# A last 1x1 convolution in seven block products, one engine for the sample copies, and a reordered opening

## The chip, the core and the metric

The kernel runs on one core of a Trainium2 chip: TensorE (PE; its weight loads are PEld) for matmuls, VectorE (DVE), ScalarE (ACT) and GpSimd (POOL) for the rest, SyncE (SP) to issue DMAs. The metric is the device time of one execution in microseconds. Each engine works through its own queue in order and waits there for semaphores.

## The reference

Two bottleneck layers run on x of 64 images, 1024 channels, 14x14, in float32.

```python
# layer 0
out = relu(bn(conv(x, w1)))                  # 1024 -> 256, 1x1
out = relu(bn(conv(out, w2, pad=1)))         # 256 -> 256, 3x3
out = bn(conv(out, w3))                      # 256 -> 1024, 1x1
x   = relu(x + softplus(residual_scale) * out)
# layer 1: a deformable bottleneck with group norms (32 groups)
out = relu(group_norm(conv(x, w1)))          # 1024 -> 256, 1x1
om  = conv(out, w_off, pad=1) + b_off        # 27: nine offsets x, nine y, nine masks
py, px = grid_y + om[9:18], grid_x + om[:9]
sampled = bilinear_sample(out, py, px) * sigmoid(om[18:])   # for each of 9 taps
out = einsum('bckhw,ock->bohw', sampled, w2)
out = relu(group_norm(out))
out = group_norm(conv(out, w3))              # 256 -> 1024, 1x1
return relu(out + x)
```

Layer 0 normalises over the batch, so each of its convolutions must be done before the next; layer 1 normalises inside one image.

## The kernel before

Images go in pairs (NP = 32 pairs, N2 = 392 = 2 x 196 columns). Channels lie on the 128 partitions: 1024 channels are CB = 8 blocks, 256 are MB = 2. The first layer is three stages over the whole batch and ends at about 967 us; nothing of it is changed.

The second layer (`build_second_bottleneck`) works on pairs in slots. Slot t holds the sampling and second convolution of pair t, the first convolution, first norm, offset convolution and sampling weights of pair t+1, and the second norm, third convolution, third norm and store of pair t-1. `slot(t)` writes out the order of TensorE's work by hand: `put(steps, extra, at)` inserts extra steps ahead of numbered steps, `weave(a, b)` mixes two lists evenly. The other engines' orders are made by a planner from the same list, except where `keep_in_program_order` holds an instruction in place.

The stages, as the steps of the list name them:

- `first_conv` (L1038): 16 products for a pair; ScalarE copies the two banks out (L1046) and VectorE takes statistics (L936). `first_norm` sums groups on TensorE (L960, L979), takes the power -0.5 on GpSimd (L985), makes scale and shift on VectorE (L991 to L1001), rectifies on ScalarE (L1062), and GpSimd copies into `pad` (L1069).
- `offset_conv` (L1082): 18 products in four column groups into one bank, added up by ScalarE and VectorE (L1092 to L1097). `selection` makes the mask, and sends offsets and mask through DRAM, so that they come back spread over taps and rows. `factors` makes the one-dimensional weights of the bilinear sampling (L1139 to L1146) and sends them out. `spread` brings them back as S and X (DMAs, L1212 and L1216), and `corners` multiplies the two on VectorE (L1234).
- `transposes` (L1175) puts the rectified rows on the partitions as aT; `lend` copies the part that the middle rows share by DMA.
- `sampling` (L1252): for each of two tap sets (five taps and four), three groups of rows, two channel blocks and one or two images, matmuls of S with aT. A bank holds up to 420 columns; two banks (`ps_s`) take turns. Each bank is copied to sm: even turns by ScalarE (L1264), odd ones by VectorE (L1262).
- `second_conv` (L1285): 36 products for a pair (72 passes in the trace), over both tap sets into two banks. `second_norm` is the first norm's twin with the rectification at L1314, in place in h2.
- `third_conv` (L1342): eight output blocks, each two products of 392 columns; ScalarE copies the bank to z (L1351), VectorE takes statistics. `third_norm` and `finish` end with z*scale + y on VectorE (L1373) and the rectification on ScalarE (L1381); `store` writes z out.
- `residual` (L212, L221) ends the first layer for pair t+2.

The banks of the third convolution, first convolution, offset convolution and transposes come from one pool of three (`ps`), in turn. S, X, sm, aT, z and h2 come from the pool `two`, of two buffers for each tag. `fill()` opens the second layer: first convolutions of pairs 0, 1 and 2, with the weights of pairs 0 and 1 as far as the slots that follow need them. `tail()` ends the last pair.

Of the kernel before, what the change touches and what calls it, by code (L numbers as in the profile page):

```python
# [16 lines left out]
P = 128  # L17
# [5 lines left out]
MB = 2  # L23
# [21 lines left out]
def kernel(  # L45
# [830 lines left out]
    def build_second_bottleneck(l1, path, run, early):  # L876
        groups, R, tapsets = path.groups, path.rows, path.tapsets
        QR = R * W
        starts = sorted({r0 for _, _, chunks in groups for r0 in chunks})
        KT = max(k1 - k0 for k0, k1 in tapsets)  # L880
        wide = sum((h1 - h0) * W * 2 * len(chunks) for h0, h1, chunks in groups)
        NS = len(starts)

# [283 lines left out]
        def transposes(p):  # L1167
            q = pairs[p]

            def step(i, c):  # L1170
                if i == c == 0:
                    q["aT"] = two.tile([QR, 2, MB, NS, P], FP, tag="aT", name=f"aT_{p}")
                pt = ps.tile([QR, 2, P], FP, tag="ps", name=f"tr_{p}_{i}_{c}")
                for j, r0 in enumerate((starts[0], starts[-1])):
                    nc.tensor.transpose(  # L1175
                        pt[:, j, :], q["a1"][:, c, ds(i * HW + r0 * W, QR)], ident
                    )
                nc.vector.tensor_copy(q["aT"][:, i, c, :: NS - 1], pt)

            return [lambda i=i, c=c: step(i, c) for i in range(2) for c in range(MB)]  # L1180
# [57 lines left out]
        def sampling(p, e):  # L1238

            q = pairs[p]  # L1240
            k0, k1 = tapsets[e]
            kt = k1 - k0
            out = []

            def step(turn, g, h0, h1, chunks, c, i0, ni):
                if turn == 0:
                    q["sm"][e] = two.tile([P, MB, KT, 2, HW], FP, tag="sm", name=f"sm_{p}_{e}")
                n = (h1 - h0) * W
                pt = ps_s.tile([P, ni, kt, n], FP, tag="ps_s", name=f"sp_{p}_{e}_{g}_{c}_{i0}")
                for i in range(ni):  # L1250
                    for j, r0 in enumerate(chunks):
                        nc.tensor.matmul(  # L1252
                            pt[:, i],
                            q["aT"][:, i0 + i, c, starts.index(r0), :],
                            q["S"][e][g, r0][:, :, i0 + i, :],
                            start=(j == 0),
                            stop=(j == len(chunks) - 1),
                        )
                for i in range(ni):
                    dst = q["sm"][e][:, c, :kt, i0 + i, h0 * W : h1 * W]  # L1260
                    if turn % 2:
                        nc.vector.tensor_copy(dst, pt[:, i])  # L1262
                    else:
                        nc.scalar.copy(dst, pt[:, i])  # L1264
# [41 lines left out]
        def second_norm(p):  # L1306
            q = pairs[p]

            def end():
                n = q["gn2"]  # L1310
                n.finish()
                for c in range(MB):
                    for i in range(2):
                        nc.scalar.activation(  # L1314
                            q["h2"][:, c, ts(i, HW)],
                            q["h2"][:, c, ts(i, HW)],
                            AF.Relu,
                            bias=n.sh[:, c, i : i + 1],
                            scale=n.sc[:, c, i : i + 1],
                        )  # L1320

            return [lambda: q["gn2"].mean(), end]

        def parts(p):

            return ((0, 4), (4, 6), (6, 8)) if p == NP - 1 else ((0, CB),)

        def third_conv(p):
            q = pairs[p]

            def step(o, c):
                half, b = divmod(o, HB)
                if o == c == 0:
                    q["z"] = []
                    q["gn3"] = [
                        Norm(b1 - b0, 1, N3S, N3B, f"gn3_{p}_{b0}", b0) for b0, b1 in parts(p)
                    ]
                if b == c == 0:
                    q["z"].append(two.tile([P, HB, N2], FP, tag="z", name=f"z_{p}_{half}"))
                if c == 0:  # L1340
                    q["pt3"] = ps.tile([P, N2], FP, tag="ps", name=f"d3_{p}_{o}")
                nc.tensor.matmul(  # L1342
                    q["pt3"],
                    w3b_sb[:, c, ts(o, P)],
                    q["h2"][:, c, :],
                    start=(c == 0),
                    stop=(c == MB - 1),
                )
                if c == MB - 1:
                    z = q["z"][half][:, b, :]  # L1350
                    nc.scalar.copy(z, q["pt3"])  # L1351
                    n = [n for n in q["gn3"] if n.b0 <= o][-1]
                    n.stats(o - n.b0, z)

            return [lambda o=o, c=c: step(o, c) for o in range(CB) for c in range(MB)]

# [55 lines left out]
        def slot(t):  # L1412
# [27 lines left out]
            om = part(front, offset_conv, t + 1) + part(front, selection, t + 1)  # L1440
            om_at = (2,) * (MB * T) + (4,)
            if d1:
                todo = put(d1, norm2 + weights[:1], (4, 8, 10) if back else (10,))
                todo += put(weave(sp[0], d3[: 2 * HB]), norm1 + weights[1:], (4, 9, 12))
                todo += put(weave(sp[1], d3[2 * HB :]), om, om_at)
            else:
                todo = weights[:1]
                todo += put(sp[0], norm2 + weights[1:], (2, 6, 7) if back else (7,))
                todo += put(weave(sp[1], d3[: 2 * HB]), norm1, (1, 4))
                todo += put(d3[2 * HB :], om, om_at)  # L1450
# [9 lines left out]
            if front:  # L1460
# [7 lines left out]
        def tail():  # L1468

            p = NP - 1  # L1470
            for step in second_norm(p):
                step()
            d3 = third_conv(p)

            def products(first, end):
                for step in d3[first:end]:
# [157 lines left out]
```

## Time and profile before

| | us |
|---|---|
| median of three runs | 3069.08 (3066.68 to 3069.61) |
| the profiled execution, its own time | 3069.61 |
| its span in the trace | 3067.7 |
| second layer's opening, to the first full slot | 967 to 1130 |
| slots 2 to 30 | 1130 to 2970 |
| last slot and tail | 2970 to 3068 |

The span is the stretch between the first and the last traced instruction. In the rows of groups and of the timeline, "x" is a count and a matmul of float32 operands stands as two passes; a bracket tells how long the engine was idle just before and what ended that. The ends of TensorE's rows are modelled, so differences of starts are the better measure of what a matmul costs.

### The profile page before, as it was taken

To read this page: it belongs to the slowest core of one execution; us is meant where nothing else is said; L and a number is where in the kernel's file an instruction comes from. 1 tells how busy PE (TensorE), PEld (TensorE's weight loads), DVE (VectorE), ACT (ScalarE), POOL (GpSimd) and SP (SyncE) were. 2 spreads that over 40 slices of the span, in tenths; PEclk is the share of its full clock that TensorE was granted. 3 is DMA by queue.
4 is the path that set the end of the run, shared out by engine and by line. 5 is a ranking of instruction groups with operands and counts; after the bars stand their busy time and mean duration, and the time that the engine had idled before them with its cause. 6 is when DMAs were issued, how large, how long until landed. Compare 5 with 4: busy or idle time off the path is not lost.

```text
span 3067.7 us, 33283 instructions
## 1 busy us (share of the span) xinstructions
PE 2985.4 (97%) x10521; PEld 1718.6 (56%) x10521; DVE 1988.7 (65%) x5321; ACT 1113.2 (36%) x2367; POOL 695.2 (23%) x631
## 2 busy tenths in 40 slices
PE   9999999989999799999999999999999999999997
PEld 5555555545555455555555555555555555555554
DVE  7877999988887355555555555555555555555554
ACT  0000212215554244443444434444344444444433
POOL 4621566646663010010000101010010100101000
PEclk9999999999999999999999999999999999999998
DMA  7654000025554444455544554445544455444531
GB/s 229 192 171 125 14 1 0 1 91 217 217 215 147 147 127 128 137 162 168 165 129 140 162 172 156 134 143 160 174 148 135 147 161 179 138 135 153 159 102 43
DMA packets 350398, 423.93 MB, mean 138 GB/s; under 512 B 27876, under 2 KB 292612, under 8 KB 349956
## 3 DMA queue, kind: packets, MB, share of 16 engines
q1 hardware_dynamic: 350212, 421.71, 43.3%
q8 instruction: 85, 1.39, 0.2%
q14 instruction: 101, 0.83, 0.1%
HBM read 296.63 MB, written 116.76 MB: 135 GB/s over the span
## 4 chain that ended last, share of the span: by engine, by line
PE 86%; DVE 11%; ACT 1%; issue 1%; DMA 1%; POOL 0%; SPq 0%; DVEq 0%; ACTq 0%; POOLq 0%
PE pd L1285 25%; PE d L1038 11%; PE sp L1252 11%; PE c L382 10%; PE d L1342 9%; PE c L763 8%; PE c L527 5%; PE om L1082 4%; DVE v L513 3%; DVE om L1094 1%; DVE sm L1262 1%; PE tr L1175 1%; PE c L728 1%; DVE off L1097 1%; DVE st L579 1%
## 5 line engine op out<-in xcount | busy, mean ns | idle before, releaser
L1285 PE MATMUL pd<-sm,w2b_sb 128*128 128x392 f32 x2304 | 791.4, 493 | 0.0
L1285 PEld LDWEIGHTS pd<-sm,w2b_sb 128*128 128x128 f32 x2304 | 425.8, 190 | 275.7
L1252 PE MATMUL sp<-S,aT 126*128 126x420 f32 (+3 forms) x1536 | 502.9, 426 | 28.1 <-ACT sm L1264 11.9
L1342 PE MATMUL d<-h,w3b_sb 128*128 128x392 f32 x1024 | 421.4, 496 | 3.2 <-ACT h L1314 3.2
L1252 PEld LDWEIGHTS sp<-S,aT 126*128 126x128 f32 x1536 | 257.2, 191 | 215.6 <-DVE sm L1262 37.5
L1038 PE MATMUL d<-h,w1b_sb 128*128 128x392 f32 x1024 | 359.7, 501 | 3.0 <-ACT h L221 3.0
L527 PE MATMUL c<-v,u_sb 128*128 128x392 f32 x1024 | 343.0, 497 | 9.4 <-DVE bn1sh L167 8.2
L985 POOL TENSOR_TENSOR gn_0sc<-gn_0sc,mhalf 128x16 f32<-128x16 f32 (+2 forms) x34 | 93.5, 2750 | 876.3 <-DVE gn_0sc L984 861.8
L527 PEld LDWEIGHTS c<-v,u_sb 128*128 128x128 f32 x1024 | 194.6, 191 | 157.8 <-issue 11.7
L936 DVE BATCH_NORM_STATS2 gn_0st<-z 128x6 f32<-128x196 f32 x504 | 159.7, 354 | 160.5 <-ACT z L1351 160.5
L1038 PEld LDWEIGHTS d<-h,w1b_sb 128*128 128x128 f32 x1024 | 190.4, 191 | 130.7 <-ACT h L221 5.2
L1342 PEld LDWEIGHTS d<-h,w3b_sb 128*128 128x128 f32 x1024 | 191.0, 191 | 120.1 <-issue 69.8
L1381 ACT ACTIVATE z<-z,gn_0sh 128x196 f32<-128x196 f32 x504 | 181.2, 444 | 138.7 <-DVE gn_0sh L1001 134.8
L1264 ACT COPY sm<-sp 128x336 f32<-128x336 f32 (+3 forms) x384 | 148.4, 404 | 212.4 <-PE sp L1252 209.9
L1262 DVE COPY sm<-sp 128x336 f32<-128x336 f32 (+3 forms) x384 | 173.2, 459 | 66.2 <-PE sp L1252 64.3
L513 DVE TENSOR_TENSOR v<-t 128x392 f32<-128x392 f32 x256 | 191.5, 806 | 0.0
L1351 ACT COPY z<-d 128x392 f32<-128x392 f32 x256 | 123.4, 482 | 149.5 <-PE d L1342 149.5
L1373 DVE SCALAR_TENSOR_TENSOR z<-z,gn_0sc,h 128x196 f32<-128x196 f32 x504 | 173.8, 421 | 0.0
L382 PE MATMUL c<-xc,w1a_sb 128*128 128x392 f32 x384 | 149.1, 497 | 5.0 <-DMA xc<-in_x_dram 5.0
L221 ACT ACTIVATE h<-h,bn3sh 128x392 f32<-128x392 f32 x256 | 140.5, 621 | 7.0 <-DVE h L212 6.4
L212 DVE SCALAR_TENSOR_TENSOR h<-h,bn3sc,h 128x392 f32<-128x392 f32 x256 | 140.7, 622 | 0.0
L715 DVE BATCH_NORM_STATS2 st<-o 128x6 f32<-128x392 f32 x256 | 127.8, 555 | 17.8 <-ACT o L746 9.2
(784 smaller groups left out, 3572.5 us busy)
## 6 DMA issues: line engine op xcount, KB each, us to landing
xc<-in_x_dram SPq DMA_DIRECT2D x128, 392.0 KB
h<-o SPq DMA_DIRECT2D x64, 784.0 KB
h<-in_x_dram SPq DMA_DIRECT2D x64, 784.0 KB
h<-h SPq DMA_DIRECT2D x64, 784.0 KB
out_dram<-z SPq DMA_DIRECT2D x126, 392.0 KB
X<-wd SPq DMA_DIRECT2D x64, 413.4 KB
S<-wd SPq DMA_DIRECT2D x64, 413.4 KB
X<-wd SPq DMA_DIRECT2D x64, 330.8 KB
```

The costliest lines, as they stand in the source:

```text
L382: nc.tensor.matmul(acc[m], a, b, start=(j == 0), stop=(j == HB - 1))
L513: nc.vector.tensor_tensor(v[:, u].rearrange("p (i y x) -> p i y x", y=7, x=7), cols[c][:, :, i : i + 13 : 2, :], cols[c][:, :, j : j + 13 ...
L527: nc.tensor.matmul(m[u], u_sb[:, c, u, k % 4, ts(o, P)], vts[k][c][:, u], start=(c == 0), stop=(c == MB - 1),)
L763: nc.tensor.matmul(planes(acc[m]), a, b, start=start, stop=True, skip_group_check=True)
L936: nc.vector.bn_stats(self.st[:, b, i, :], src[:, ts(i, HW)])
L1038: nc.tensor.matmul(q["pt"][o], w1b_sb[:, c, ts(o, P)], q["y"][:, c, :], start=(c == 0), stop=(c == CB - 1),)
L1252: nc.tensor.matmul(pt[:, i], q["aT"][:, i0 + i, c, starts.index(r0), :], q["S"][e][g, r0][:, :, i0 + i, :], start=(j == 0), stop=(j == len ...
L1262: nc.vector.tensor_copy(dst, pt[:, i])
L1285: nc.tensor.matmul(q["pd"][o], w2b_sb[:, c, k, ts(o, P)], q["sm"][e][:, c, k - k0].rearrange("p i q -> p (i q)"), start=(k == 0 and c == 0 ...
L1342: nc.tensor.matmul(q["pt3"], w3b_sb[:, c, ts(o, P)], q["h2"][:, c, :], start=(c == 0), stop=(c == MB - 1),)
L1373: nc.vector.scalar_tensor_tensor(z[:, ts(i, HW)], z[:, ts(i, HW)], n.sc[:, b, i : i + 1], q["y"][:, o, ts(i, HW)], ALU.mult, ALU.add,)
L1381: nc.scalar.activation(z[:, ts(i, HW)], z[:, ts(i, HW)], AF.Relu, bias=n.sh[:, b, i : i + 1])
```

## The change

The third convolution of all pairs but the last uses a 2x2 block scheme with seven products in place of eight. Weights are blocks a11 to a22 (channel block by half of the outputs, four sub-blocks of 128 each), the input blocks b11 to b22 are channel block by image. Four combined weights are made once by GpSimd. Four combinations of the input are made by GpSimd after each second norm. For each quarter j there are seven products of 196 columns in three banks; ScalarE, VectorE and GpSimd combine them into four blocks of z. The last pair keeps the plain scheme on the combined weights.

The copies of sampling banks are all made by ScalarE, two images of a small group in one instruction. S, X and sm come from the pool `one`, with a tag for each set; aT of this path too. In a slot the second norm's end stands one step earlier. `fill` no longer makes the weights and transposes of pair 1, which go into slot 0; it does the residual of pair 2 and the mask's selection earlier, the product of the first weights inside the third first convolution, and touches the sigmoid once at its start.

The diff, cut to its core:

```diff
+    a11, a12, a21, a22 = (w3b_sb[:, c, ts(o, 512)] for o in range(2) for c in range(2))
+    Sb = {n: const.tile([P, 512], FP, tag=f"Sb{n}", name=f"Sb{n}") for n in (1, 2, 4)}
+    Sb[3] = a21
+    for n, a, b, op in (
+        (1, a21, a22, ALU.add),
+        (2, Sb[1], a11, ALU.subtract),
+        (3, a11, a21, ALU.subtract),
+        (4, a12, Sb[2], ALU.subtract),
+    ):
+        nc.gpsimd.tensor_tensor(Sb[n], a, b, op)
...
-                    q["aT"] = two.tile([QR, 2, MB, NS, P], FP, tag="aT", name=f"aT_{p}")
+                    q["aT"] = (one if len(tapsets) == 2 else two).tile([QR, 2, MB, NS, P], FP, tag="aT", name=f"aT_{p}")
...
-            S = two.tile([QR, wide * KT], FP, tag="S", name=f"S_{p}_{e}")
-            X = two.tile([QR, wide * KT], FP, tag="X", name=f"X_{p}_{e}")
+            S, X = (
+                one.tile([QR, wide * KT[e % 2]], FP, tag=f"{v}{e % 2}", name=f"{v}_{p}_{e}")
+                for v in ("S", "X")
+            )
...
-                for i in range(ni):
-                    dst = q["sm"][e][:, c, :kt, i0 + i, h0 * W : h1 * W]
-                    if turn % 2:
-                        nc.vector.tensor_copy(dst, pt[:, i])
-                    else:
-                        nc.scalar.copy(dst, pt[:, i])
+                dst = q["sm"][e][:, c, :kt, i0 : i0 + ni, h0 * W : h1 * W]
+                nc.scalar.copy(dst, pt.rearrange("p i k n -> p k i n"))
...
+                T3 = q["T3"] = {
+                    m: one.tile([P, HW], FP, tag=f"T{m}", name=f"T{m}_{p}") for m in (1, 2, 4)
+                }
+                (b11, b12), (b21, b22) = ([h2[:, c, ts(i, HW)] for i in range(2)] for c in range(2))
+                nc.gpsimd.tensor_tensor(T3[1], b12, b11, ALU.subtract)
+                nc.gpsimd.tensor_tensor(T3[2], b22, T3[1], ALU.subtract)
+                nc.gpsimd.tensor_tensor(b12, b22, b12, ALU.subtract)
+                nc.gpsimd.tensor_tensor(T3[4], b21, T3[2], ALU.subtract)
...
+                a, b = (
+                    (a11[:, o], b11),
+                    (Sb[1][:, o], T3[1]),
+                    (Sb[2][:, o], T3[2]),
+                    (Sb[3][:, o], b12),
+                    (a12[:, o], b21),
+                    (Sb[4][:, o], b22),
+                    (a22[:, o], T3[4]),
+                )[m]
+                if m in (0, 2, 4):
+                    q["bank", m // 2] = ps.tile([P, 2, HW], FP, tag="ps", name=f"d3_{p}_{j}_{m}")
+                bank = q["bank", 1 if m == 6 else m // 2]
+                nc.tensor.matmul(bank[:, m % 2 if m < 6 else 1], a, b, start=(m < 6), stop=True, skip_group_check=True)
+                z = [q["z"][half][:, j, :] for half in range(2)]
+                if m == 1:
+                    q["E"] = one.tile([P, 2, HW], FP, tag="E", name=f"E_{p}_{j}")
+                    nc.scalar.copy(q["E"], bank)
+                elif m == 3:
+                    V = q["V"] = one.tile([P, 2, HW], FP, tag="V", name=f"V_{p}_{j}")
+                    E = q["E"]
+                    nc.vector.tensor_tensor(V, bank, E, ALU.add)
+                    nc.gpsimd.tensor_tensor(E[:, 1], V[:, 0], E[:, 1], ALU.add)
+                    nc.gpsimd.tensor_tensor(z[1][:, HW:], V[:, 0], V[:, 1], ALU.add)
+                elif m == 5:
+                    nc.vector.tensor_tensor(
+                        z[0].rearrange("p (i n) -> p i n", i=2), bank, q["E"], ALU.add
+                    )
+                    third_stats(p, j)
+                elif m == 6:
+                    nc.vector.tensor_tensor(z[1][:, :HW], bank[:, 1], q["V"][:, 0], ALU.add)
+                    third_stats(p, HB + j)
+            return [lambda j=j, m=m: step(j, m) for j in range(HB) for m in range(7)]
...
-                todo = put(d1, norm2 + weights[:1], (4, 8, 10) if back else (10,))
-                todo += put(weave(sp[0], d3[: 2 * HB]), norm1 + weights[1:], (4, 9, 12))
-                todo += put(weave(sp[1], d3[2 * HB :]), om, om_at)
+                todo = put(d1, norm2 + weights[:1], (4, 7, 10) if back else (10,))
+                todo += put(weave(sp[0], d3[: len(d3) // 2]), norm1 + weights[1:], (4, 9, 12))
+                todo += put(weave(sp[1], d3[len(d3) // 2 :]), om, om_at)
...
-            first = put(pd[0], part(front, transposes, t + 1), (3, 6, 9, 12))
-            first = put(first, part(front, factors, t + 1), (3, 8))
+            first = put(pd[0], part(ahead, transposes, t + 1), (3, 6, 9, 12))
+            first = put(first, part(ahead, factors, t + 1), (3, 8))
...
+            nc.scalar.activation(one.tile([32, 1], FP, tag="m", name="table"), boff_sb[:32], AF.Sigmoid)
             steps = first_conv(0, by_inputs=True)
             steps += put(
                 first_conv(1),
-                first_norm(0) + offset_conv(0) + [lambda: residual(2)] + selection(0) + factors(0),
-                (3, 6) + (12,) * (MB * T) + (12, 15, 16, 16),
+                first_norm(0) + [lambda: residual(2)] + offset_conv(0) + selection(0) + factors(0),
+                (3, 6, 7) + (12,) * (MB * T) + (12, 16, 16),
             )
...
                 first_conv(2),
-                first_norm(1) + offset_conv(1) + selection(1) + factors(1) + transposes(1),
-                (2, 5) + (12,) * (MB * T) + (14,) + (16,) * 6,
+                first_norm(1) + [lambda: corners(0, 0)] + offset_conv(1) + selection(1),
+                (2, 5, 10) + (12,) * (MB * T) + (14,),
             )
-            steps += [lambda: lend(1), lambda: corners(0, 0)]
```

More of the change, by code (lines that the diff above doesn't have):

```diff
@@ L879, in build_second_bottleneck @@
         starts = sorted({r0 for _, _, chunks in groups for r0 in chunks})
-        KT = max(k1 - k0 for k0, k1 in tapsets)
+        KT = [max(k1 - k0 for k0, k1 in tapsets[n::2]) for n in range(2)]
         wide = sum((h1 - h0) * W * 2 * len(chunks) for h0, h1, chunks in groups)
@@ L1246, in step @@
                 if turn == 0:
-                    q["sm"][e] = two.tile([P, MB, KT, 2, HW], FP, tag="sm", name=f"sm_{p}_{e}")
+                    q["sm"][e] = one.tile(
+                        [P, MB, KT[e % 2], 2, HW], FP, tag=f"sm{e % 2}", name=f"sm_{p}_{e}"
+                    )
                 n = (h1 - h0) * W
@@ L1311, in end @@
                 n.finish()
+                h2 = q["h2"]
                 for c in range(MB):
@@ L1314, in end @@
                         nc.scalar.activation(
-                            q["h2"][:, c, ts(i, HW)],
-                            q["h2"][:, c, ts(i, HW)],
+                            h2[:, c, ts(i, HW)],
+                            h2[:, c, ts(i, HW)],
                             AF.Relu,
@@ L1320, in end @@
                         )
+                if p == NP - 1:
+                    return
+                T3 = q["T3"] = {
[6 more added lines that the diff above has]
+                nc.gpsimd.tensor_tensor(T3[4], b21, T3[2], ALU.subtract)
             return [lambda: q["gn2"].mean(), end]
@@ L1326, in parts, with first_of_third, third_stats @@
             return ((0, 4), (4, 6), (6, 8)) if p == NP - 1 else ((0, CB),)
+        def first_of_third(p):
+            q = pairs[p]
+            q["z"] = [
+                two.tile([P, HB, N2], FP, tag="z", name=f"z_{p}_{half}") for half in range(2)
+            ]
+            q["gn3"] = [
+                Norm(b1 - b0, 1, N3S, N3B, f"gn3_{p}_{b0}", b0) for b0, b1 in parts(p)
+            ]
+        def third_stats(p, o):
+            q = pairs[p]
+            n = [n for n in q["gn3"] if n.b0 <= o][-1]
+            n.stats(o - n.b0, q["z"][o // HB][:, o % HB, :])
@@ L1328, in third_conv, with step @@
         def third_conv(p):
             q = pairs[p]
+            def step(j, m):
+                if j == m == 0:
+                    first_of_third(p)
+                h2, T3, o = q["h2"], q["T3"], ts(j, P)
+                (b11, b12), (b21, b22) = ([h2[:, c, ts(i, HW)] for i in range(2)] for c in range(2))
+                a, b = (
[24 more added lines that the diff above has]
+                        z[0].rearrange("p (i n) -> p i n", i=2), bank, q["E"], ALU.add
+                    )
+                    third_stats(p, j)
+                elif m == 6:
+                    nc.vector.tensor_tensor(z[1][:, :HW], bank[:, 1], q["V"][:, 0], ALU.add)
+                    third_stats(p, HB + j)
@@ L1331, in step, with plain_third_conv @@
+            return [lambda j=j, m=m: step(j, m) for j in range(HB) for m in range(7)]
+        def plain_third_conv(p):
+            q = pairs[p]
             def step(o, c):
-                half, b = divmod(o, HB)
                 if o == c == 0:
[L1334 to L1339, printed above, removed]
+                    first_of_third(p)
+                    d = q["E"] = one.tile([P, N2], FP, tag="E", name=f"E_{p}")
+                    nc.vector.tensor_tensor(d, q["h2"][:, 1], q["h2"][:, 0], ALU.subtract)
@@ L1340, in step @@
                 if c == 0:
                     q["pt3"] = ps.tile([P, N2], FP, tag="ps", name=f"d3_{p}_{o}")
[L1342 to L1348, printed above, removed]
+                j = ts(o % HB, P)
+                a, b = (
+                    ((a11[:, j], q["h2"][:, 0]), (a12[:, j], q["h2"][:, 1]))
+                    if o < HB
+                    else ((Sb[1][:, j], q["h2"][:, 0]), (a22[:, j], q["E"]))
+                )[c]
@@ L1349, in step @@
+                nc.tensor.matmul(q["pt3"], a, b, start=(c == 0), stop=(c == MB - 1))
                 if c == MB - 1:
[L1350 to L1353, printed above, removed]
+                    nc.scalar.copy(q["z"][o // HB][:, o % HB, :], q["pt3"])
+                    third_stats(p, o)
             return [lambda o=o, c=c: step(o, c) for o in range(CB) for c in range(MB)]
@@ L1448, in slot @@
                 todo += put(sp[0], norm2 + weights[1:], (2, 6, 7) if back else (7,))
-                todo += put(weave(sp[1], d3[: 2 * HB]), norm1, (1, 4))
-                todo += put(d3[2 * HB :], om, om_at)
-            first = put(pd[0], part(front, transposes, t + 1), (3, 6, 9, 12))
-            first = put(first, part(front, factors, t + 1), (3, 8))
+                todo += put(weave(sp[1], d3[: len(d3) // 2]), norm1, (1, 4))
+                todo += put(d3[len(d3) // 2 :], om, om_at)
+            first = put(pd[0], part(ahead, transposes, t + 1), (3, 6, 9, 12))
+            first = put(first, part(ahead, factors, t + 1), (3, 8))
             first = put(first, norm3, (2, 13))
@@ L1459, in slot @@
                 todo += [lambda e=e: spread(t + 1, e) for e in range(min(2, E))]
-            if front:
+            if ahead:
                 todo.append(lambda: lend(t + 1))
@@ L1472, in tail @@
                 step()
-            d3 = third_conv(p)
+            d3 = plain_third_conv(p)
             def products(first, end):
```

## Prediction

> **What bounds the kernel now.** I read the page first, then the busy time by stage, then one pair of the second layer on each engine.
>
> ```profile
> span 3067.7 us, 33283 instructions
> PE 2985.4 (97%) x10521; PEld 1718.6 (56%) x10521; DVE 1988.7 (65%) x5321; ACT 1113.2 (36%) x2367; POOL 695.2 (23%) x631
> ```
>
> TensorE is busy 97% of the span and the chain that ended last runs over it for 86%. The change touches only the second layer, so the stages decide:
>
> ```profile
> 967.00:1130.00 163.00, 141.33 (x520) 77.19 (x521) 77.78 (x233) 56.98 (x120) 12.53 (x13) 0.95 0.35 115
> 1130.00:2970.00 1840.00, 1829.32 (x6950) 1061.32 (x6949) 1041.97 (x3472) 772.35 (x1731) 172.16 (x145) 1.00 0.48 151
> ```
>
> (Columns: stretch, length, busy PE, PEld, DVE, ACT, POOL, granted clock.) From 1130 us on, 29 slots follow each other with TensorE idle 10 us in all; in the chain their long second convolutions start at 1177.98, 1241.55, 1305.13: every 63.57 us. Only there can fewer products pay, and only there can a new wait cost 29 times. The opening, 967 to 1130, leaves TensorE idle for 22 us.
>
> TensorE inside one slot:
>
> ```profile
> 1395.32 0.87 PE L1252 MATMUL sp<-S,aT 126*128 126x420 f32 x2
> 1396.03 0.82 PE L1342 MATMUL d<-h,w3b_sb 128*128 128x392 f32 x2
> 1396.69 0.87 PE L1252 MATMUL sp<-S,aT 126*128 126x420 f32 x2
> ...
> 1401.01 0.64 PE L1252 MATMUL sp<-S,aT 126*128 126x140 f32 x4
> 1401.49 0.28 PE L979 MATMUL gn_7p<-gn_7v,grp_sb 128*128 128x4 f32 x2
> ...
> 1416.40 0.59 PE L1252 MATMUL sp<-S,aT 126*128 126x112 f32 x4
> 1417.36 0.70 PE L1252 MATMUL sp<-S,aT 126*128 126x112 f32 x4 [0.37 <-DVE sm L1262]
> ```
>
> Take differences of starts, not durations. A product over 392 columns (two passes in the trace) takes 0.66 us, a 420-column sampling step 0.705. Four passes of 140 columns take 0.48, 0.12 each, so passes with new weights can follow at least that fast.
>
> **The change, part by part.**
>
> *Fewer columns.* Per pair 16 products of 392 columns (16 x 0.658 = 10.53 us) become 28 of 196. No 196-column row exists. The columns alone give 0.331 us for two passes; the weight-load rows (190 ns each) would give 0.38 if they bound. Since passes of 140 columns came every 0.12 us behind such loads, I take 0.331: 9.27 us, **a gain of 1.26 us per slot**. At 0.38 it is 10.64, no gain.
>
> *What the combinations need.* Per quarter j: ScalarE copies two products (E, 0.48 by the 392 row), VectorE adds V and z0 (PSUM, 392: 0.565) and half of z1 (0.36, between its 168- and 392-column PSUM rows), GpSimd does two adds of 196. The eight z copies and half the sampling copies go. VectorE loses about 5.5 us of copies and gets about 6 us of adds; ScalarE adds roughly 2 us. Neither is near full. The new thing is order: E is finished by GpSimd, z0 waits for it, and the next j needs the banks. GpSimd's adds:
>
> ```profile
> L778 POOL TENSOR_TENSOR w<-e,e 128x392 f32<-128x392 f32 x56 | 56.9, 1017 | 78.3 <-ACT e L777 74.8 <-DVE st L715 3.5
> L331 POOL TENSOR_TENSOR e<-g 128x192 f32<-128x192 f32 x8 | 4.7, 589 | 0.0
> ```
>
> [...] The rows say 0.51 (half of 1.017) to 0.59. [...] The four input differences after the second norm take 4 x 0.55 = 2.2 us on GpSimd. The norm now ends one step (0.66 us) earlier; its rectifications end 1.8 us before the first product, and the differences are ready at or before that product. Free; without this cover they cost up to 2.2.
>
> *Sampling copies on ScalarE alone.* The trace shows what stands in that queue:
>
> ```profile
> 1402.57 1.01 POOL L985 TENSOR_TENSOR gn_7sc<-gn_7sc,mhalf 128x4 f32<-128x4 f32 x1 [11.10 <-DVE gn_7sc L984]
> ...
> 1403.76 0.51 ACT L1264 COPY sm<-sp 128x420 f32<-128x420 f32 x1 [1.61 <-PE sp L1252]
> 1405.08 1.87 ACT L1062 ACTIVATE a<-a,gn_7sh,gn_7sc 128x196 f32<-128x196 f32 x4 [0.81 <-DVE gn_7sh L1001]
> 1406.86 0.46 ACT L1351 COPY z<-d 128x392 f32<-128x392 f32 x1
> ```
>
> The rectification of the next pair's first norm waits on ScalarE for VectorE and GpSimd. Before, VectorE emptied every second sampling bank meanwhile. [...] I walk the queues in the changed program's order, from the first product at 0, with these durations and hand-overs of 0.05 us (0.15 into GpSimd, 0.2 out of TensorE).
>
> - V of j=0 runs 3.8 to 4.3 on VectorE; GpSimd's two adds end at 5.6; VectorE's next instruction, statistics of that half of z1, waits for them and ends at 6.0. The norm's sum on TensorE was ready at 4.9, but its VectorE step stands behind: 6.1. The power on GpSimd (1.01) ends at 7.2, z0 and statistics interleave, the shift is ready at 8.35, and z1 of j=0, queued after it, ends at 8.65.
> - TensorE is ready at 7.75 for j=1's third product, whose bank waits for that z1: **0.95 us**.
> - ScalarE rectifies 8.4 to 10.3, and only then copies the sampling step issued before: 10.55. TensorE wants that bank at 9.0: **1.6 us**. In the kernel before, other copies stood there.
> - The offset convolution takes the bank that z1 of j=1 releases, again behind a GpSimd add: **0.5 us**.
> - The third norm's mean comes two products into the second convolution. VectorE's last work (GpSimd's half, z0, z1, statistics, sum) ends at about 29.5, 2.1 us after that convolution starts, where 1.3 are granted: **0.75 us**.
>
> Sum 3.8 us. What goes: the waits on copies of VectorE (the 0.37 shown above and some 0.3 in a pair of sampling steps). Per slot -1.26 - 0.7 + 3.8 = **+1.85 us**; done for the kernel before, the same walk ends 0.7 us before the measured 38.48 us from first convolution to second and puts its waits where the trace has them. 29 slots: **+53 us**.
>
> *Single buffers.* S, X and sm were two buffers rotating over two tap sets: the same buffer comes back for the same set, so no new wait. aT becomes single; its writer runs inside the second convolution, after the samplings that read it. z's two halves are now both claimed early, but the stores were issued about 25 us before. Nothing; if a store were late, below 1 us per slot.
>
> *Opening.* Four of its idle spells:
>
> ```profile
> 1001.03 0.69 PE L1175 MATMUL tr<-ident,a 128*126 128x128 f32 x2 [4.54 <-DVE aT L1178]
> ...
> 1022.51 7.05 PE L1252 MATMUL sp<-S,aT 126*128 126x420 f32 x22 [1.50 <-DVE S L1234]
> 1036.77 9.55 PE L1252 MATMUL sp<-S,aT 126*128 126x420 f32 x26 [7.21 <-ACT sm L1264]
> ...
> 1035.47 0.86 ACT L1140 ACTIVATE wt<-wt 126x784 f32<-126x784 f32 x1 [6.94 <-DVE wt L1139]
> ```
>
> The 4.54 is eight residual steps (4.4 us) ahead of the transposes' copies on VectorE; they move up, leaving about 1.5. The convolution behind it took 17.2 us where its starts elsewhere add to 14.3; most of that returns. The table load (1.28 us) leaves the mask's path. The first sampling then waits for the spread weights: SP issues the next residual's load ahead of the offsets' store now, and the weights' 12 transfers after it, so I let them come only 6 us earlier (1016, between 1013 and 1021). The 7.21 is ScalarE waiting for pair 1's weights; that work goes behind the sampling copies, with its four transposes (0.9 us) into the second convolution. SP still issues pair 1's round trip after pair 0's 12 transfers, so the last copies may meet it at 1030; I count the wait as gone. Second convolution at about 1030 instead of 1046, less 0.9: **-15 us** (-7 if only that wait goes, -19 if all do). The four weight sums on GpSimd (about 1.3 us each) lie in its idle 7 us before 980. Slots 1 and 31, with seven-product quarters back to back without sampling between, get about +3 (0 to 6); the tail's one subtraction is hidden.
>
> Sum: 3069.6 (profiled execution, span 3067.7 plus 1.9; the median of the three is 3069.1) + 53 - 15 + 3 = **3110 us**.
>
> **The rivals.**
>
> 1. *The waits shrink, and the change is faster.* One mechanism: GpSimd's adds. [...] If the planner's order lets the shift of the first norm come 1.5 us sooner, ScalarE's wait goes and with it both big stalls: slot -0.7, total -32, 3037. For it: TensorE is the bound and its work falls. Against: every row of 192 elements and more is slower than 0.5. Chance 0.19, at about 3055.
> 2. *The opening's gain eats the slots' loss*: slot +0.5, total about 3071. Chance 0.05.
> 3. *Main forecast, slot +1.0 to +2.4*: 3085 to 3130. Chance 0.64.
> 4. *Weight loads bind narrow products* (0.38 us): 1.4 us more per slot, 29 x 3.2 + 3 - 15 = +81, 3150; or GpSimd adds at 0.76 (its slowest 192 row): slot +3.1, the same size. Chance 0.12.
>
> That it does not do what it says is excluded for the products: the changed program has 28 narrow matmuls per pair.
>
> **The numbers.** Likeliest 3110. Range 3062 to 3134: it leaves out rival 4 and the deeper half of rival 1. This kernel's repeats lie within 3 us, so 0.2% (6 us) is about what can be told. Faster 0.19, same 0.05, slower 0.76.
>
> **What the profile after would show.** The products' line with 196 columns and starts 0.33 us apart; GpSimd adds near 0.55; in each slot a wait of about 1.6 us of sampling on ScalarE's copy just after the first norm's rectification, one near 1 us of a product on VectorE's z1, 0.5 at the offset convolution, 0.75 at the third norm's mean; a slot period of 65.4; slot 2 starting near 1115 instead of 1130. Wrong if the period is below 63.6: then the rectification came in time.

## The result, and the profile after

The changed kernel takes 3112.31 us (median of 4 runs, 3111.03 to 3115.03), the kernel before 3069.18 on the same chip: ratio 1.0143, 95% interval 1.0126 to 1.0161. It is slower by 43 us; the prediction said 3110. That the number is so near is luck: the slots cost less than predicted and the opening gained far less, and the two errors largely cancel.

The head of the page after, and the busy time by the two stretches of the second layer (stretch, length, busy PE, PEld, DVE, ACT, POOL, then the granted clock, the busy share of the DMA engines and their GB/s):

```profile
span 3109.1 us, 35631 instructions
PE 2946.9 (95%) x11265; PEld 1820.2 (59%) x11265; DVE 2044.9 (66%) x5310; ACT 1192.8 (38%) x2500; POOL 962.6 (31%) x1007
967.00:1130.00 163.00, 141.19 (x555) 79.90 (x554) 80.56 (x227) 64.79 (x134) 26.28 (x33) 0.98 0.39 125
1130.00:2970.00 1840.00, 1754.27 (x7464) 1132.98 (x7462) 1071.70 (x3401) 824.48 (x1806) 411.19 (x484) 1.00 0.48 149
```

TensorE does less work (2985 to 2947 us) and is idle more: 86 us in the slots, where it was 11. The waits of TensorE from 1130 to 3000 us (what waited, for what, us in all, times, longest) name the two places:

```profile
PE sp L1270 <- ACT sm L1278: 61.7, 29, 2.1
PE gn_0p L973 <- DVE gn_0m L964: 26.7, 29, 0.9
```

In the timeline of TensorE in one slot they look like this (start, duration, what, in brackets the idle time before it and what ended it):

```profile
1405.01 0.64 PE L1270 MATMUL sp<-S,aT 126*128 126x140 f32 x4
...
1405.83 0.87 PE L1270 MATMUL sp<-S,aT 126*128 126x420 f32 x2
1406.54 0.50 PE L1392 MATMUL d<-T,Sb 128*128 128x196 f32 x2
1409.15 0.97 PE L1270 MATMUL sp<-S,aT 126*128 126x420 f32 x2 [2.12 <-ACT sm L1278]
...
1428.82 0.39 PE L973 MATMUL gn_0p<-gn_0m,grp_sb 128*128 128x16 f32 x2 [0.92 <-DVE gn_0m L964]
```

ScalarE at that time, from its own timeline:

```profile
1404.55 0.39 ACT L1278 COPY sm<-sp 128x280 f32<-128x280 f32 x1 [0.53 <-PE sp L1270]
1406.95 1.88 ACT L1075 ACTIVATE a<-a,gn_7sh,gn_7sc 128x196 f32<-128x196 f32 x4 [2.01 <-DVE gn_7sh L1014]
1408.73 0.37 ACT L1278 COPY sm<-sp 128x280 f32<-128x280 f32 x1
1409.01 0.48 ACT L1396 COPY E<-d 128x392 f32<-128x392 f32 x1
```

ScalarE idled 2.01 us at the head of its queue, waiting for the norm's shift; then it rectified for 1.88. The bank of turn 5 (the four passes of 140 columns at 1405.01) was complete from about 1405.7 on, but its copy stood behind in the queue. TensorE still made the step of turn 6 (1405.83), in the other bank; the step of turn 7 needed the bank of turn 5 and started when its copy was done (1409.15). ScalarE is busy 38% of the span: its order is the trouble, not its load.

Where the 41.4 us between the two spans lie, by the starts of the second convolutions on TensorE:

| stretch | before | after | difference |
|---|---|---|---|
| start to slot 1's second convolution | 1104.65 | 1101.59 | -3.1 |
| from there 29 slots on | 1843.97 | 1887.38 | +43.4 |
| the rest | 119.1 | 120.1 | +1.0 |

The slot period is 64.97 us where it was 63.57; two of the 29 slots took 66.65.

### The profile page after: what moved, and what is told of

It reads as the page before. It is cut to its first block, busy times and chain, and to the rows that moved or that the text cites. A ratio compares the mean times of both kernels' runs of the same rounds, so it can differ in the third digit from the quotient of the medians.

```text
span 3109.1 us, 35631 instructions
## 1 busy us (share of the span) xinstructions
PE 2946.9 (95%) x11265; PEld 1820.2 (59%) x11265; DVE 2044.9 (66%) x5310; ACT 1192.8 (38%) x2500; POOL 962.6 (31%) x1007
## 4 chain that ended last, share of the span: by engine, by line
issue 21%; PE 21%; DVE 9%; POOL 8%; ACT 4%; DMA 3%; SPq 0%; POOLq 0%; DVEq 0%; ACTq 0%
PE sp L1270 7%; PE d L1392 5%; PE pd L1299 4%; DVE h L212 4%; PE om L1095 3%; POOL gn_0sc L998 3%; DVE gn_0st L949 2%; ACT h L1329 2%; ACT a L1075 2%; POOL h L1345 1%; POOL z L1402 1%; DMA h<-in_x_dram 1%; POOL E L1401 1%; DMA S<-wd 1%; DVE V L1400 1%
## 5 line engine op out<-in xcount | busy, mean ns | idle before, releaser
L1270 PE MATMUL sp<-S,aT 126*128 126x420 f32 (+3 forms) x1536 | 494.8, 419 | 73.6 <-ACT sm L1278 67.4
L1278 ACT COPY sm<-sp 128x336 f32<-128x336 f32 (+3 forms) x640 | 288.7, 452 | 284.1 <-PE sp L1270 271.9
L1401 POOL TENSOR_TENSOR E<-V,E 128x196 f32<-128x196 f32 x124 | 74.1, 598 | 516.0 <-DVE V L1400 512.2
L1250 DVE TENSOR_TENSOR S<-S,X 126x840 f32<-126x840 f32 (+1 forms) x192 | 169.2, 920 | 9.3 <-DMA S<-wd 9.3
L1392 PE MATMUL d<-h,w3b_sb 128*128 128x196 f32 x744 | 164.4, 329 | 0.7 <-DVE z L1404 0.7
L1392 PEld LDWEIGHTS d<-h,w3b_sb 128*128 128x128 f32 x744 | 132.7, 189 | 40.8 <-issue 19.6
```

Of the source, the lines that this page charges most:

```text
L1270: nc.tensor.matmul(pt[:, i], q["aT"][:, i0 + i, c, starts.index(r0), :], q["S"][e][g, r0][:, :, i0 + i, :], start=(j == 0), stop=(j == len ...
L1278: nc.scalar.copy(dst, pt.rearrange("p i k n -> p k i n"))
L1392: nc.tensor.matmul(bank[:, m % 2 if m < 6 else 1], a, b, start=(m < 6), stop=True, skip_group_check=True)
```

## Experiments

All ratios are against the kernel before on the same chip. The period is that of the undisturbed slots, from the starts of second convolutions.

| run | time, us | ratio, 95% interval | period, us |
|---|---|---|---|
| changed | 3112.31 | 1.0143 (1.0126 to 1.0161) | 64.97 |
| 1 copies alternating | 3159.22 | 1.0292 (1.0278 to 1.0306) | 65.65 |
| 2 sums issued late | 3112.08 | 1.0143 (1.0127 to 1.0158) | 64.97 |
| 3 mean later | 3103.55 | 1.0110 (1.0095 to 1.0126) | 64.24 |
| 4 before, new opening | 3063.03 | 0.9982 (0.9975 to 0.9989) | 63.58 |
| 5 before, copies on ScalarE | 3075.24 | 1.0025 (1.0015 to 1.0035) | 63.80 |
| 6 alternating, S x X later | 3116.95 | 1.0154 (1.0140 to 1.0167) | 64.97 |
| 7 sums pinned late | 3107.46 | 1.0128 (1.0112 to 1.0143) | 64.97 |
| 8 = 6 + 7 + mean later | 3095.20 | 1.0087 (1.0073 to 1.0101) | 64.45 |
| 9 rectification in parts | 3061.66 | 0.9975 (0.9966 to 0.9985) | 63.33 |
| 10 = 9 + 7 + mean later | 3035.00 | 0.9890 (0.9875 to 0.9905) | 62.60 |

**1. Copies alternating again.**

```
-                nc.scalar.copy(dst, pt.rearrange("p i k n -> p k i n"))
+                if turn % 2:
+                    nc.vector.tensor_copy(dst, pt.rearrange("p i k n -> p k i n"))
+                else:
+                    nc.scalar.copy(dst, pt.rearrange("p i k n -> p k i n"))
```

> The changed kernel, with the sampling copies alternating between ScalarE and VectorE again, everything else as changed. Theory (the slot grew because the copy that frees a sampling bank queues on ScalarE behind the first norm's rectification): TensorE's wait of 2.1 us for that copy goes from each of 29 slots, so 29 x 2.1 = 61 us go, about 3051 us, slot period 62.9. Rival (it is the combination of the seven products on VectorE and GpSimd, or the narrower products themselves, that cost): the wait moves to VectorE's copies or to z, which has the more to do by 9 copies of 0.35 to 0.5 us a slot; no more than 10 us go, 3100 us or more.

Measured: 3159 us, the opposite. The pause is still there. ScalarE, VectorE and TensorE, from their timelines in one slot:

```profile
1484.94 1.87 ACT L1075 ACTIVATE a<-a,gn_8sh,gn_8sc 128x196 f32<-128x196 f32 x4 [1.42 <-DVE gn_8sh L1014]
1486.73 0.46 ACT L1399 COPY E<-d 128x392 f32<-128x392 f32 x1
1487.09 0.50 ACT L1281 COPY sm<-sp 128x420 f32<-128x420 f32 x1
...
1485.62 1.91 DVE L1250 TENSOR_TENSOR S<-S,X 126x672 f32<-126x672 f32 x3
1487.45 0.44 DVE L1279 COPY sm<-sp 128x280 f32<-128x280 f32 x1
...
1487.64 1.25 PE L1270 MATMUL sp<-S,aT 126*128 126x420 f32 x2 [2.03 <-ACT sm L1281]
```

Both banks are late. Turn 5's copy is on VectorE now, and there it stands behind S x X and starts at 1487.45. That work is put at place 12 of a woven list that has grown from 18 to 24 items, so it comes earlier against the sampling than in the kernel before. Turn 6's copy is on ScalarE, still behind the rectification, and ends at 1487.59. TensorE resumed at 1487.64 on ScalarE's copy, before VectorE's had ended (1487.89): here turn 7 took the bank of turn 6. So the theory, in the form "give VectorE its copies back", fell: the rectification still held the bank that TensorE took. Against the changed kernel the period is 0.68 longer, 0.30 of it the wait for the third norm's mean (1.22 instead of 0.92), and 13 slots of 29 instead of two lose another 1.7 us each, to the granted clock (see run 3).

**2. Weight sums issued late.** The four sums were moved into slot 0's second convolution in the program, without pinning them.

> The changed kernel, with the four weight sums on GpSimd issued in the middle of slot 0's second convolution instead of ahead of the second layer. Theory (the four sums of 1.25 us hold up VectorE's small operations and the residual of pair 0, and through them TensorE's start of the second layer's first convolution): the wait of 4.2 us for h before the product L1051 shrinks, the first convolution's norm starts about 6.4 us sooner, 3106 us. Rival (that start is late for the loading of h or the last norms of the first layer): no change, 3112 us.

Measured: no change. It tested nothing: the planner makes GpSimd's order, and it left the sums where they were, at the end of the first layer, as GpSimd's timeline shows:

```profile
972.77 1.26 POOL L877 TENSOR_TENSOR Sb<-w3b_sb 128x512 f32<-128x512 f32 x1
```

**3. Third norm's mean later.**

```
-            first = put(first, norm3, (2, 13))
+            first = put(first, norm3, (6, 15))
```

> The changed kernel, with the product of the third norm's mean two products and two transposes later (and the next of that norm two places later too). Theory: TensorE's wait of 0.9 us for gn_0m goes from 29 slots, 27 us, 3086 us, slot period 64.05. Rival (the norm then ends later and its rectification delays ScalarE's copies for the next slot, or the transposes' copies on VectorE take the wait): within 8 us of 3112.

Measured: 3103.55, a third of the gain expected. The wait of 0.92 is gone and the period is 64.24 (-0.73), but 11 of the 29 slots take 65.8 to 65.9. The busy time by stretches, in one of them:

```profile
1402.00:1406.00 4.00, 4.00 (x25) 3.51 (x24) 1.86 (x7) 1.41 (x3) 1.91 (x3) 1.00 0.77 311
1406.00:1410.00 4.00, 1.87 (x8) 1.14 (x7) 3.60 (x12) 2.68 (x7) 1.52 (x3) 0.96 0.03 10
1410.00:1412.00 2.00, 2.00 (x6) 1.38 (x5) 0.07 (x1) 0.76 (x2) 0.27 (x1) 0.50 0.00 0
1412.00:1414.00 2.00, 2.00 (x7) 1.39 (x6) 0.67 (x2) 0.41 (x1) 1.15 (x2) 0.72 0.00 0
```

The third number from the end is the granted clock. Behind the pause of 2.13 us (1407.4 to 1409.5) it falls to 0.50 for 3.4 us, and 1.7 us are lost. The changed kernel makes the same pause of 2.12 us in every slot and pays this in two of 29. So a shift of the pause by less than a microsecond decides whether it costs 2.1 or 3.8 us; the last section shows what it is measured against. Run 1 pays it too: slots of 65.65 and of 67.33 alternate over most of it.

**4. The kernel before with the new opening alone** (the new fill, the transposes of pair 1 in slot 0, the early table load).

> The kernel before, with the new order of the opening alone (table loaded early, residual and corners earlier, transposes of pair 1 in slot 0), two-half products, alternating copies and no weight sums as before. Theory: the opening between the first norm's mean and slot 0's second convolution shortens by 13 us, of which slot 0 gives back 1 and slot 1 some 2: 3058 us. Rival (the gain is of the other parts, or is given back in the slots): within 4 us of 3069.

Measured: 3063.03, so the opening is a gain, of 5 us by the times. In the profiled runs slot 0's second convolution starts at 1037.36 instead of 1046.16 and the span is 9.2 us shorter; that profiled run lies near the low end of 20 runs (3059.8 to 3065.9). The 13 us were too many. The first sampling now waits for S x X instead:

```profile
PE sp L1252 <- DVE S L1234: 6.2, 2, 4.0
```

**5. The kernel before with its copies on ScalarE alone.** Edit: the copy of the changed kernel in place of the two branches.

> The kernel before with one edit: all sampling copies on ScalarE, one instruction a bank (its two-half products, their copies and everything else as before). Theory (a sampling copy on ScalarE queues behind the 1.87 us of the first norm's rectification and holds TensorE whatever form the products have): a wait of 1.5 to 2.1 us a slot for that copy, less the 0.4 us for VectorE's copy that goes; 29 x 1.1 to 1.7 = 32 to 49 us more, 3101 to 3118 us, and 1.7 us more for each slot in which the granted clock falls to 0.5 behind the wait. Rival (the wait is special to the seven products, which leave the sampling less to hide behind): 3055 to 3075 us.

Measured: 3075.24, between the two. The rectification starts 8.31 us after the first product, as in the changed kernel (8.35), but the bank it holds is one turn later. ScalarE and TensorE:

```profile
1403.36 0.39 ACT L1260 COPY sm<-sp 128x280 f32<-128x280 f32 x1 [0.31 <-PE sp L1252]
1405.31 1.88 ACT L1062 ACTIVATE a<-a,gn_7sh,gn_7sc 128x196 f32<-128x196 f32 x4 [1.56 <-DVE gn_7sh L1001]
1407.10 0.48 ACT L1260 COPY sm<-sp 128x420 f32<-128x420 f32 x1
...
1407.63 0.97 PE L1252 MATMUL sp<-S,aT 126*128 126x420 f32 x2 [0.92 <-ACT sm L1260]
```

Turn 5 got through at 1403.36; only turn 6 is held. The pause is 0.92, the old 0.37 and smaller ones go, and the period is 0.23 longer. So the copies alone are a small part. The 2.12 needs them together with the seven products, whose steps bring turn 5 to ScalarE just behind the rectification.

**6. Alternating copies with S x X behind turn 7.**

```
-                todo += put(weave(sp[0], d3[: len(d3) // 2]), norm1 + weights[1:], (4, 9, 12))
+                todo += put(weave(sp[0], d3[: len(d3) // 2]), norm1 + weights[1:], (4, 9, 18))
```

> The changed kernel with the sampling copies alternating and the weights of the second tap set (the S x X products on VectorE, 1.9 us) six places later, behind the copies of turns 5 and 7. Theory (in the run with alternating copies alone VectorE's copy of turn 5 stood behind S x X just as ScalarE's stands behind the rectification, so the pause stayed): the wait of 2.0 us shrinks to 0.5 or less, the clock doesn't fall, the slot period is 63.2, about 3061 us. Rival (the combination on VectorE leaves it no room for the copies): a wait of 1.5 us or more stays, 3100 us or more.

Measured: 3116.95. The pause is broken up and the slots with a low clock are gone, yet the period is the same 64.97; that it is the same to the hundredth is chance. The waits of TensorE from 1130 to 3000 us:

```profile
PE gn_0p L973 <- DVE gn_0m L964: 35.7, 29, 1.6
PE sp L1270 <- DVE sm L1279: 14.0, 29, 0.5
PE d L1395 <- DVE V L1403: 12.3, 29, 0.4
PE sp L1270 <- ACT sm L1281: 5.6, 29, 0.2
```

From the first sampling step to the offset convolution a slot is 0.76 us shorter than in the changed kernel, from there to the second convolution 0.46 longer, and the second convolution 0.31 longer. VectorE has V, z0, half of z1 and the statistics already, and ten copies in between make those late. The rival was right about the engine and wrong about the form: in place of one wait of 1.5 us there are four, and the longest, for the mean, is 1.22 in 28 of the 29 slots. Run 8 (expected 3031) confirms it:

> The changed kernel with all the repairs: alternating copies, S x X six places later, the third norm's mean later, weight sums pinned in slot 0. Theory: 1.7 + 0.9 us a slot and 6 us in the opening go: 3112 - 29 x 2.6 - 6 = 3031 us, slot period 62.3, ahead of both kernels. Rival (with one wait gone another engine is late, as in the run with the late mean, where the granted clock fell to 0.5 in every third slot): 3060 us or more.

Measured: 3095.20. Both repairs that work elsewhere are in it, and with alternating copies it is still behind the kernel before.

**7. Weight sums pinned.** Each sum was issued with `tc.keep_in_program_order` behind the copies of pair 1 into the padded image; they ran from 1011.5 to 1016.6, ahead of the first sampling.

> The changed kernel with the four weight sums on GpSimd pinned behind the copies of pair 1 into the padded image, that is, in slot 0's second convolution. (In the earlier run with late sums the program's order on GpSimd was unchanged: they still ran at 973 to 978 us.) Theory: VectorE's small operations L166 and L815 take 0.16 and 0.22 us again, TensorE's wait of 4.2 us for h ahead of L1051 goes, and the second layer starts 6 us sooner, 3106 us. Rival (TensorE is late there for something else, or the gain is lost again at the first sampling, which waits for S): 3111 us or more.

Measured: 3107.46, 4.9 us less than the changed kernel; in the profiled runs slot 0's second convolution starts 5.1 us sooner (1035.90, not 1040.97). What the sums did where the change had put them, from the timelines of GpSimd, VectorE and TensorE in the changed kernel:

```profile
975.13 1.26 POOL L876 TENSOR_TENSOR Sb<-w3b_sb 128x512 f32<-128x512 f32 x1
...
975.16 1.25 DVE L166 TENSOR_TENSOR bn3sh<-bn3mv,bn3sc 128x4 f32<-128x4 f32 x1
976.52 1.24 DVE L815 TENSOR_SCALAR bn3sc<-bn3sc,spr 128x4 f32<-128x4 f32 x1
977.68 1.30 DVE L815 TENSOR_SCALAR bn3sh<-bn3sh,spr 128x4 f32<-128x4 f32 x1
...
981.30 9.12 PE L1051 MATMUL d<-h,w1b_sb 128*128 128x392 f32 x22 [4.24 <-ACT h L221]
```

and VectorE in run 7:

```profile
974.07 0.16 DVE L166 TENSOR_TENSOR bn3sh<-bn3mv,bn3sc 128x4 f32<-128x4 f32 x1
974.35 0.22 DVE L815 TENSOR_SCALAR bn3sc<-bn3sc,spr 128x4 f32<-128x4 f32 x1
974.48 0.22 DVE L815 TENSOR_SCALAR bn3sh<-bn3sh,spr 128x4 f32<-128x4 f32 x1
```

Operations over four elements take as long as the GpSimd add beside them. They feed the residual of pair 0, and that the first convolution. The wait of 4.24 is gone in run 7.

**9. The rectification in two parts.** All copies stay on ScalarE; only the queue changes. The rectification's instructions (`rectify(c, i)`, each issued in program order) become list entries of their own, two behind turn 6, two behind turn 7:

```
-  norm1 + weights[1:], (4, 9, 12))
+  norm1 + weights[1:], (4, 9) + (16, 16, 18, 18) * (len(norm1) > 2) + (12,))
```

> The changed kernel, all sampling copies on ScalarE as changed, with the four instructions of the first norm's rectification issued in two twos: two behind the copy of turn 6, two behind that of turn 7, so that the copy of turn 5 no longer queues behind the whole 1.88 us. Theory (it is the order in ScalarE's queue, not its load, that holds TensorE): the wait of 2.1 us goes or shrinks below 0.4, slot period 62.9 to 63.3, 3051 to 3064 us, ahead of the kernel before. Rival (ScalarE has too much to do in this stretch with ten copies, so the wait moves to a later copy, or the offset convolution now waits for the padded image, which comes 1 us later): a wait of 1 us or more a slot stays, 3080 us or more.

Measured: 3061.66, 51 us less than the changed kernel and ahead of the kernel before. This decides between the theories: the engines, the copies and the products are the same, only the order in ScalarE's queue differs. What is left, by the waits from 1130 to 3000 us:

```profile
PE gn_0p L973 <- DVE gn_0m L964: 27.6, 30, 0.9
PE om L1105 <- DVE z L1414: 19.9, 29, 0.7
```

The second is the offset convolution waiting for z1 of j=1, hidden behind the pause until now.

**10. All that works.** Run 9, the late mean, the pinned sums.

> As the run with the rectification in parts, and the third norm's mean later and the weight sums pinned in slot 0. Theory: the three are independent; the late mean is worth 0.73 a slot where the granted clock doesn't fall (the period of the earlier run with the late mean in undisturbed slots was 64.23 against 64.97), the sums 5 us: 29 x 0.73 + 5 = 26 us less than the run with the parts alone, 3025 to 3038 us, slot period 62.2, no slot with a lowered clock. Rival (the mean moved later makes the third norm's rectification late, a wait elsewhere): less than 10 us under the run with the parts alone.

Measured: 3035.00, 34 us ahead of the kernel before and the best of all. The head of its page, then ScalarE's timeline in one slot, with copies between the two parts of the rectification:

```profile
span 3032.0 us, 35573 instructions
PE 2939.1 (97%) x11265; PEld 1827.0 (60%) x11265; DVE 2029.7 (67%) x5310; ACT 1189.7 (39%) x2500; POOL 974.8 (32%) x1007
```

```profile
1394.12 0.51 ACT L1290 COPY sm<-sp 128x420 f32<-128x420 f32 x1 [0.18 <-PE sp L1282]
1394.53 0.99 ACT L1074 ACTIVATE a<-a,gn_7sh,gn_7sc 128x196 f32<-128x196 f32 x2
1395.43 0.49 ACT L1290 COPY sm<-sp 128x420 f32<-128x420 f32 x1
1395.82 0.99 ACT L1074 ACTIVATE a<-a,gn_7sh,gn_7sc 128x196 f32<-128x196 f32 x2
```

TensorE is at 97% again. The slot period is 62.60 us, and none of the 29 slots is lengthened by the clock; slot 1, ahead of them, is, by a stretch at 0.50 from 1073.4 to 1076.8. The same late mean that was worth 9 us in run 3 brings its full 0.73 a slot here, because no pause is left for the clock to fall in: from 1780 to 2900 us TensorE's longest is 0.70.

## Why the prediction was right, and where it was not

Right in sign, size and main mechanism, wrong in the sum of waits and in the opening. That 3110 lies 2 us from the measurement is luck: the loss in the slots was put 10 us too high, and the gain of the opening 12 us too high.

- *Fewer columns, -1.26 us a slot.* Right. Passes of 196 columns start 0.33 us apart for two. 63.57 - 1.26 - 0.37 (the old wait on VectorE's copy) + 2.12 + 0.92 = 64.98, measured 64.97. Run 10 against run 4 differs by -0.98 a slot; -1.26 - 0.37 + 0.69 (the wait left) is -0.94. Rival 4, weight loads that bind, is out.
- *The sampling step behind the rectification.* The cause and the place were right: shift ready 8.31 us after the first product (predicted 8.35), turn 5's copy behind the rectification. The division was wrong: 0.95 for the third product of j=1 plus 1.6 for the sampling were predicted, and one wait of 2.12 came. That third product started at 1406.54, ahead of the end of z1 of j=0 (VectorE, 1406.82 to 1407.18): it did not get the bank the walk had given it. The walk assumed a strict rotation of the banks. The trace fits a pool that hands out the bank released first, as does turn 7 in run 1; no run tested that alone.
- *Offset convolution, 0.5.* Did not appear, since the pause had let VectorE catch up; it appears as 0.69 in runs 9 and 10. *Third norm's mean, 0.75*: 0.92.
- *Slots, +53.* Measured +43.4 (a period of 65.4 was predicted, 64.97 came), of which 3.4 are the two slots with a lowered clock, which the prediction did not have. The step that failed is the sum of waits: 3.8 predicted, 3.04 measured, partly offset by the old waits, put at 0.7, where 0.37 is what the waits of before show.
- *Opening, -15.* Measured -3.1 with slot 1, and the first layer ended 1.5 us later in this profile. Two terms failed. The weight sums were costed at nothing because GpSimd was idle there; run 7 shows 4.9 us, through VectorE. And the first sampling was taken to find S at 1016; it started at 1025.33, after a wait of 2.62 for S x X. Run 4 puts the reordering itself at 5 us by the times, 9 by the profile. Nor does the sum have the granted clock. The convolution that took 17.2 us where its starts elsewhere add to 14.3 (it started at 1001.51) began in one of its low stretches:

```profile
999.90:1006.73 6.83, 5.70 (x12) 3.38 (x13) 4.04 (x16) 3.64 (x6) 0.00 (x0) 0.50 0.94 296
```

From 967 us to slot 1's second convolution TensorE was busy for 13.2 us at a clock of 0.50 before (999.90 to 1006.73, 1034.02 to 1040.85, 1081.80 to 1085.22) and for 6.7 after (981.2 to 984.6, 1025.5 to 1028.9). Half of the difference, 3.3 us, is an estimate of what the clock alone gave back, about as much as the whole 3.1.
- *GpSimd's work.* The adds were put at 0.55. Measured 0.598 (x124): nearer the 192-column row, 0.589, than the halved 392 row. The four input differences took 3.5 us, not 2.2 (1395.86 to 1399.34 in one slot), and were free all the same. Single buffers showed no wait on TensorE in the slots; the last slot and tail took 1.0 us more.
- *Rival 1* held that the shift of the norm might come earlier and bring about 3037. It didn't come earlier, but taking its rectification out of the copies' way, with the late mean and the sums moved, gave 3035.

## What to carry to other kernels

When work moves to one engine, look at what waits in that engine's queue with its input not ready: everything behind it inherits its wait, whatever the engine's share of busy time. Here that share was 38%, and the copy of a bank complete at 1405.7 started at 1408.73; two instructions at a time instead of four was worth 51 us. If a list of steps grows, entries put at fixed places in it move against the rest. And an idle engine was not free cover here: beside GpSimd's sums VectorE's operations of 0.16 and 0.22 us took 1.24 to 1.30, and pinning the sums elsewhere gave 4.9 us.

## What the hardware showed that was not expected

- *A pause of 2.1 us can halve TensorE's clock, and where it falls decides.* 11 slots of run 3 and 13 of the 29 of run 1 ran 3.4 us at a granted clock of 0.50, 1.7 us lost each time; the changed kernel did so in 2 slots of 29 with a pause of the same length. Within a run the starts of all low stretches lie on one grid: in the changed kernel those at 1800.37 and 2776.58 are 286 times 3.413 us apart. Two cells of that grid in the changed kernel, each with the cell behind it (columns as above; the number behind the comma is TensorE's busy time):

```profile
1732.11:1735.52 3.41, 1.53 (x7) 1.21 (x8) 2.37 (x5) 3.12 (x8) 1.53 (x2) 1.00 0.01 2
1735.52:1738.94 3.42, 3.42 (x21) 2.10 (x23) 2.05 (x6) 1.32 (x3) 1.16 (x2) 1.00 0.00 0
...
1796.96:1800.38 3.42, 1.43 (x6) 1.11 (x7) 2.38 (x6) 3.15 (x8) 1.53 (x2) 1.00 0.00 2
1800.38:1803.79 3.41, 3.41 (x8) 2.07 (x7) 1.75 (x5) 0.60 (x2) 1.15 (x2) 0.50 0.01 2
```

With TensorE idle for 1.88 us of a cell the clock stayed, with 1.99 it fell for the next cell. Over the 29 slots of all twelve kernels the line lies between 1.95 and 1.96 us: no cell with less idle time was followed by a low one, and each of the 30 with more was. (The ends of TensorE's rows are modelled, and in the openings, where the rows have other shapes, the line is less sharp: 1.73 us was enough in two runs, and in run 2 about 2.0, in the cell of the pause that ended at 1066.54, was not.) So in these runs a pause of 2.12 us cost the clock only where nearly all of it fell into one cell. A slot of 64.97 us is 19.03 cells, so from slot to slot the pause moves by 0.11 us against the grid, and the two low stretches lie 15 slots apart; run 3's 64.24 us are 18.82 cells, which brings the pause to such a place every second or third slot. That the changed kernel paid only twice is luck of its period. What sets the grid, and why 1.96 us of a cell are enough, no run shows.
- *GpSimd and VectorE hold each other up.* VectorE operations of 0.16 and 0.22 us took 1.25 and 1.24 to 1.30 beside GpSimd adds of 1.26. In each of the 29 slots of the changed kernel S x X took 3.13 us beside the four input differences, and the third of these (L1345) 1.39; in slot 1, where the two lie apart, they took 2.32 and 0.60. What in the two engines makes them wait for each other no run shows.
